# Deformable-convolution kernel: hats eight rows behind their offsets, the search for far pixels between the last hats, and another order at sampling's start

## The chip, the cores and the metric

The kernel runs on one core of one Trainium2 chip. The metric is the device time of one execution in microseconds (us), the median of several executions. The engines are TensorE (PE: matmuls and transposes; PEld is its weight load), VectorE (DVE), ScalarE (ACT), GpSimd (POOL) and SyncE (SP, which here only issues transfers, reads a register and branches). Each engine works through its own queue of instructions in order; an instruction that waits holds up everything behind it in the same queue. The kernel is written with a tile framework: a tile belongs to a tag with a number of buffers, and an instruction that writes a reused buffer waits until the last reader of the old contents is done. When a pool is closed and another takes its space, the first users of the new one wait for the last users of the old.

## The reference

`x` is `[2, 256, 128, 128]` in float32. Two residual blocks follow one another:

```
x = x + L0(gn(x))           # gn: GroupNorm with 32 groups
x = x + L1(gn(x))

L0(x):  for dil in (1, 9, 12):
            off = conv3x3(x, w_off, 18 channels, dilation dil)
            y   = sum over 9 taps k of w_def[c,k] *
                  bilinear(x, at pixel + tap k * dil + off[k])   # 0 outside
            branch = gelu(layernorm over channels(y) * bw + bb)
        out = ln(sum of branches + conv1x1(x) + b)
        out = ln(mlp(out) + out)                      # 256 -> 512 gelu -> 256
L1(x):  conv3x3(x, ternary weights) + bias
```

The offsets are small for the data at hand but may be anything: a sampled point further than two pixels from its tap's place is a far pixel and must still come out right.

## The kernel before

**Statistics and phase A** (0 to about 938 us). For each of the two images, its GroupNorm statistics are taken (L529), then `phase_a` (L321) goes over 32 groups of R = 4 rows. `columns(g)` loads the rows (`xa`, issued on ACT's queue, L340), normalises them on the DVE (L207), transposes them on PE (L350), copies them out of PSUM on ACT (L355), stores them as a zero-padded table in DRAM for sampling (SP, L356), multiplies them by all taps of the three offset convolutions (`pz`, PE, L364) and copies the product into a ring of 40 rows (`zr`, L371; the rows alternate between DVE and ACT). As soon as the ring holds the rows that eight rows of offsets need (twelve further down, the largest dilation), `offsets(G)` adds the taps up on the DVE (`zs`, L398 to L412), shifts and sums them on PE (`po`, L415), copies the offsets out (`offs`, L423), subtracts the usual position (`rest`, L425), keeps the largest distance per column and row (`reach`, L428), stores the offsets (SP, L432) and splits them into three bf16 parts (`parts`, L438 to L441; two buffers, by G's parity). Then `make_hats` runs twice, once for every four rows: eight PE transposes of `parts` (`pp`, L450 and L451), two DVE copies (`planes`, L453 and L454), and six times a pair of matmuls (`ph`, L463, two PSUM banks) followed by an absolute value on ACT (`hb`, L470); after every three of them a DVE operation makes hat functions of them (L474) and SP stores them to the DRAM tensor `hats` (L475, one store of 576 KB and one of 720 KB; `hb` has three buffers). At the bottom of an image the last step of the ring brings several `offsets` with two make_hats each behind the last columns.

**The search** (`missing`, L558 to L727; 938 to 965 us) has a pool of its own. It loads tables (`aux`, `misc`, `tapid`), marks the pixels whose `reach` is over two (`V`, L580), ranks them by matmuls (`pb`, L591; `pl`, L606), and gathers three things for up to 128 of them by indirect DMA on POOL: their offsets (`of`), the vertical base positions of their row (`ybase`) and the horizontal ones of their column (`xbase`), all at L628. A long chain of small DVE operations (L644 to L724) finds the taps that the hats don't cover. If there are more of them than a fixed number, a flag is raised: `worst` is reduced over the partitions on POOL (L792), compared (L794), read into a register (L795, `beyond`), and a branch chooses between `sample_near` and a slow general path.

**Sampling** (`sample_near`, L1224; 966 to 5762 us). Its order is written out by hand: `pin` keeps an instruction in its place in the program. 396 units (image, one of 66 pairs of rows, branch) are worked through. `load_tiles` loads eleven `xs` tiles from the table for a pair of rows (L1269, 18 buffers), `load_hats(u)` loads up to three pairs `hy`, `hx` of unit u (L1295, three buffers each), `build` multiplies a pair into the interpolation matrix `A` (DVE, L1315), `sample` multiplies `xs` by `A` on PE (`pm`, L1416), ACT copies the product out (`ev`, L1428) and the DVE adds it up in a ring (L1377). `prepare(u)` builds all of unit u and then asks for the hats of unit u + 1; `sample(u, 1)` calls `prepare(u + 2)`. Image rows at the top edge have fewer taps, so units 0 to 2 have one pair of hats each and matmuls of 72 columns, later ones up to three pairs and 216. `lacking` (L729) computes what far pixels need in addition: ten indirect gathers on POOL (`G` and `dws`, L628), and some thirty DVE operations that multiply them by weights and add them up into `extra` (L735 to L771). Its result is first used when the first group of finished rows goes into the tail of layer 0.

The second block's convolution (5762 to 6694 us) is not touched.

The order at sampling's start, which the change alters, is in the code:

```
load_tiles(*units[0][0:2])
load_hats(0)
prepare(0)
prepare(1)
tail.extra = lacking(pool, tail.tile, miss)
begun_groups = 0
spot(0)
for u, (b, Rt, br) in enumerate(units):
```

Of the kernel before, what the change touches and what calls it, by code (L numbers as in the profile page):

```python
# [71 lines left out]
def conv_preact_kernel(ctx: ExitStack, tc: tile.TileContext, t: dict, out: bass.AP):  # L72
# [248 lines left out]
    def phase_a(b, pool, psum, k, beside):  # L321
# [53 lines left out]
        def offsets(G):  # L375
# [60 lines left out]
            parts = k["parts"][G % 2]  # L436
# [47 lines left out]
        for g in range(NGRP):  # L484
            columns(g)
            next(beside, None)
            while G < H // ZG and min(H - 1, G * ZG + ZG - 1 + max(DILS)) < (g + 1) * R:
                parts = offsets(G)
                for j in range(ZG // R):
                    make_hats(G * (ZG // R) + j, parts, j * R)  # L490
                G += 1

    with ExitStack() as actx:
        psum = actx.enter_context(tc.tile_pool(name="ps_a", bufs=1, space=PSUM))

        def gps():
            return psum.tile([P, 512], F32, name="gnps", tag="tp", bufs=2)

        ap = actx.enter_context(tc.tile_pool(name="apool", bufs=1))
        dxs = sorted({d * s for d in DILS for s in (-1, 0, 1)})  # L500
        k = {
            "dxs": dxs,
            "zero": ap.tile([P, C], F32, name="zero"),
            "wz": ap.tile([P, KC, NZ], F32, name="wz"),
            "shift": ap.tile([P, len(dxs), P], F32, name="shift"),
            "mid": ap.tile([P, ZG, NOFF], F32, name="mid"),
            "hatw": ap.tile([P, 2, NTAP * NH], BF16, name="hatw"),
            "parts": [ap.tile([P, 2, ZG, P], BF16, name=f"parts{i}") for i in range(2)],
            "zr": ap.tile([P, ZRING, NZ], F32, name="zr"),
            "planes": [ap.tile([P, 2, NG], BF16, name=f"planes{i}") for i in range(2)],  # L510
        }
        nc.vector.memset(k["zero"], 0.0)
        for parts in k["parts"]:
            nc.vector.memset(parts, 0.0)
        XT = min(4, NGRP)
        beside = store_signs(ap)
        for b in range(NB):
            stats = ap.tile([P, KC, NGRP, 6], F32, name=f"stats1_{b}", tag=f"stats1_{b}")
            for c in range(KC):
                for g0 in range(0, NGRP, XT):  # L520
                    xt = ap.tile([P, XT * NG], F32, name="xt", tag="xt", bufs=3)
                    nc.sync.dma_start(
                        xt,
                        x[b, c * P : (c + 1) * P].rearrange("p h w -> p (h w)")[
                            :, g0 * NG : (g0 + XT) * NG
                        ],
                    )
                    for j in range(XT):
                        nc.vector.bn_stats(stats[:, c, g0 + j, :], xt[:, j * NG : (j + 1) * NG])  # L529
            if b == 0:  # L530
                load_now()
                nc.sync.dma_start(k["wz"], t["wz"].rearrange("(k p) n -> p k n", p=P))
                nc.sync.dma_start(k["shift"], t["shift"])
                nc.sync.dma_start(k["mid"], t["mid"])
                hatw = ap.tile([P, 2, NTAP * NH], F32, name="hatw32", tag="xt", bufs=3)
                nc.sync.dma_start(hatw, t["hatw"])
                nc.vector.tensor_copy(k["hatw"], hatw)
                split_rows(ap)
                pattern = ap.tile([P, NG], F32, name="pattern", tag="xt", bufs=3)
                nc.sync.dma_start(pattern[HALF : HALF + NPAT], t["pattern"])  # L540
                for pl in k["planes"]:
                    nc.vector.tensor_copy(
                        pl[HALF : HALF + NPAT, 1, :], pattern[HALF : HALF + NPAT]
                    )
            mean, rstd = group_norm(stats, f"gn1_{b}", gps)
            gn1.append((mean, rstd))

            nc.vector.tensor_scalar(negmean[b], mean, -1.0, None, ALU.mult)
            for c in range(KC):
                nc.vector.tensor_scalar(  # L550
                    convs[b][:, c, :], convs[b][:, c, :], rstd[:, c : c + 1], None, ALU.mult
                )
            phase_a(b, ap, psum, k, beside)
        for _ in beside:
            pass


    def missing(psum, pool):  # L558
# [4 lines left out]
        def bank(name):  # L563
            return psum.tile([P, 512], F32, name=name, tag="ms", bufs=2)

        aux = pool.tile([P, NB * H + ROWS + P], F32, name="aux", tag="aux", bufs=1)
        nc.sync.dma_start(aux, t["aux"])
# [3 lines left out]
        misc = const.tile([P, 16], F32, name="misc")  # L571
        nc.sync.dma_start(misc, t["misc"])
        thirds, own_w, seq = misc[:, 0:3], misc[:, 3:4], misc[:, 4:12]
        tapid = pool.tile([P, NTAP], F32, name="tapid", tag="tapid", bufs=1)
        nc.sync.dma_start(tapid, t["tapid"])

        V = tmp("V", P, NB * H)
# [21 lines left out]
        what = pool.tile([P, 8, 2], F32, name="what", tag="what", bufs=1)  # L599
        nc.vector.tensor_copy(what[:, :, 0], top)  # L600
        nc.vector.tensor_copy(what[:, :, 1], own_w.broadcast_to([P, 8]))
        pl = bank("pl")
        for j in range(8):
            one = pool.tile([P, ROWS], F32, name="one", tag="one", bufs=2)
            nc.vector.tensor_scalar(one, slot, rank[:, j : j + 1], None, ALU.is_equal)
            nc.tensor.matmul(  # L606
                pl[0:ROWS, 0:2], lhsT=one, rhs=what[:, j, :], start=j == 0, stop=j == 7
            )
# [27 lines left out]
        gather(base[:, 0], t["ybase"], 1)  # L636
        gather(base[:, 1], t["xbase"], 2)
# [91 lines left out]
    def lacking(pool, tile_v, m):  # L729

        def quarters(name):
            return tile_v(name).rearrange("p k n -> p (k n)").rearrange("p (j c) -> p j c", c=C)

        D = quarters("D")[:, 0:3]
        nc.vector.memset(D, 0.0)  # L735
        Gs = [quarters("G") for _ in range(EACH)]
        dws = quarters("dws")
        for j in range(EACH):
            for i in range(4):
                m["gather"](Gs[j][:, i], tables, i, m["idx"][:, j])  # L740
            m["gather"](dws[:, j], t["defwt"], 4, m["idx"][:, j])
        for j in range(EACH):
            s = dws[:, EACH + j]
            for i in range(4):
                w = m["got"][:, j, i : i + 1]
                if i == 0:
                    nc.vector.tensor_scalar(s, Gs[j][:, i], w, None, ALU.mult)
                else:
                    nc.vector.scalar_tensor_tensor(s, Gs[j][:, i], w, s, ALU.mult, ALU.add)
# [474 lines left out]
    def sample_near(pool, psum, k):  # L1224
# [235 lines left out]
        for u, (b, Rt, br) in enumerate(units):  # L1460
            if br == BRS[0] and u + len(BRS) < len(units):
                load_tiles(*units[u + len(BRS)][0:2])
            for c in range(KC):
                sample(u, c)
# [463 lines left out]
```

## Time and profile before

| | us |
|---|---|
| runs: median (lowest to highest of 3) | 6704.66 (6697.62 to 6708.94) |
| the profiled execution | 6696.33 |
| its span | 6694.5 |
| PE busy | 6292.8 (94%) |
| DVE busy | 5911.4 (88%) |
| ACT busy | 4194.8 (63%) |
| POOL busy | 686.2 (10%) |
| hats stores, 64 of each size | 576 and 720 KB each |
| granted clock, mean | 0.971 of full speed |

The durations quoted come from the one profiled execution, whose own time lies 8.3 us under the median of the three runs. The span is the time from its first to its last instruction. A busy share is a mean over stages that have different limits, so the stages are looked at one by one. Behind each group of instructions the profile gives the idle time of its engine just before them, and the instruction or the transfer that ended it. "SPq" is the queue of transfers that SP issues: a row there is the time of issuing, and the landing comes later.

### The profile page before, as it was taken

What the parts mean: (1) busy time and instruction counts of PE and PEld (TensorE: products, weight loads), DVE (VectorE), ACT (ScalarE), POOL (GpSimd) and SP (SyncE); (2) the same over time, 40 slices, a digit from 0 to 9 for tenths busy, and PEclk for the clock granted to TensorE, in tenths of its full rate; (3) what the DMA queues carried; (4) which work ended last, traced back from release to release, by engine and by line L of the source; (5) the groups of instructions that cost most, each with busy time, mean ns of one, the idle gap of its engine ahead of it and who ended that gap; (6) DMA issues with size and microseconds to landing.
All of it is one profiled execution on the core that took longest, in us unless ns stands there. A gap on an engine that the chain in (4) does not pass through costs nothing.

```text
span 6694.5 us, 100612 instructions
## 1 busy us (share of the span) xinstructions
PE 6292.8 (94%) x32242; PEld 4996.0 (75%) x32242; DVE 5911.4 (88%) x13758; ACT 4194.8 (63%) x8690; POOL 686.2 (10%) x667
## 2 busy tenths in 40 slices
PE   5889968899999999999999999999999999989999
PEld 3455548888888888888888888888888888744444
DVE  7766657999999999999878999999999999689996
ACT  2334427677777777777676777777777777545442
POOL 0000010011111111111110111111111111200000
PEclk9999978999999999999999999999999999889999
DMA  8866657887777877787667787778777777343332
GB/s 294 258 198 191 198 147 197 224 222 224 223 218 216 225 218 220 219 223 216 190 190 203 220 225 221 220 216 222 224 219 220 218 222 210 120 161 132 131 144 89
DMA packets 635571, 1360.47 MB, mean 203 GB/s; under 512 B 109336, under 2 KB 290120, under 8 KB 618512
## 3 DMA queue, kind: packets, MB, share of 16 engines
q1 hardware_dynamic: 617040, 1318.90, 68.6%
q10 hardware_dynamic: 17408, 33.56, 1.5%
q8 instruction: 261, 4.28, 0.3%
q14 instruction: 286, 2.34, 0.1%
q0 software_dynamic: 576, 1.39, 0.1%
HBM read 1087.09 MB, written 266.47 MB: 202 GB/s over the span
## 4 chain that ended last, share of the span: by engine, by line
PE 56%; DVE 26%; DMA 8%; ACT 6%; issue 3%; SPq 1%; POOL 0%; ACTq 0%; DVEq 0%; POOLq 0%
PE pm L1416 25%; DVE ring L1377 11%; PE hp L857 6%; PE pc L1755 6%; PE h L1100 5%; PE pz L364 4%; DVE A L1315 4%; DMA xa<-in_x 3%; PE pc L1100 3%; DMA hx<-hats 3%; ACT ev L1428 3%; ACT v L1078 2%; PE ph L463 2%; PE tp L872 2%; DMA xs<-tables 1%
## 5 line engine op out<-in xcount | busy, mean ns | idle before, releaser
L1416 PE MATMUL pm<-A,xs 96*128 96x216 f32 (+2 forms) x17424 | 3237.6, 342 | 196.3 <-DMA xs<-tables 47.0
L1416 PEld LDWEIGHTS pm<-A,xs 96*128 96x128 f32 x17424 | 3041.3, 194 | 392.1 <-ACT ev L1428 118.2
L1377 DVE SCALAR_TENSOR_TENSOR ring<-ev,defw,ring 128x256 f32<-128x256 f32 (+4 forms) x6372 | 2482.2, 451 | 101.4 <-ACT ev L1428 51.1
L1428 ACT COPY ev<-pm 128x432 f32<-128x432 f32 (+4 forms) x4488 | 1988.2, 483 | 903.5 <-PE pm L1416 672.4
L1315 DVE TENSOR_TENSOR A<-hy,hx 96x768 f32<-96x768 f32 (+1 forms) x1124 | 1008.8, 945 | 155.7 <-PE pm L1416 83.5
L1070 POOL TENSOR_TENSOR rs<-rs,mhalf 128x4 f32<-128x4 f32 x320 | 469.1, 1466 | 4214.6 <-DVE rs L1069 3667.6
L1755 PE MATMUL pc<-cring,signs 128*128 128x512 bf16 x3456 | 758.2, 382 | 17.1 <-DMA signs<-signd 7.7
L1078 ACT ACTIVATE v<-v,rs 128x256 f32<-128x256 f32 x1280 | 694.5, 594 | 16.9 <-POOL rs L1071 16.8
L1755 PEld LDWEIGHTS <-signs 128*128 128x128 bf16 x3456 | 339.7, 98 | 434.9 <-issue 28.2
L857 PE MATMUL hp<-S,w 128*128 128x512 f32 x1024 | 504.0, 618 | 0.6 <-ACT S L1180 0.6
L1064 DVE BATCH_NORM_STATS2 st<-v 128x6 f32<-128x256 f32 x1280 | 447.0, 411 | 38.0 <-ACT v L888 38.0
L1100 PE MATMUL h<-w,hT 128*128 128x256 f32 x2048 | 477.1, 379 | 0.0
L364 PE MATMUL pz<-wz,xa 128*128 128x486 f32 x1024 | 465.0, 583 | 8.5 <-DVE zr L371 8.5
L1359 ACT ACTIVATE ring<-ev,defw 128x256 f32<-128x256 f32 (+1 forms) x856 | 404.5, 485 | 24.2
L1100 PEld LDWEIGHTS h<-w,hT 128*128 128x128 f32 x2048 | 369.3, 190 | 65.5 <-issue 1.0
L470 ACT ACTIVATE hb<-ph 96x512 f32<-96x512 f32 (+1 forms) x384 | 214.0, 593 | 185.1 <-PE ph L463 170.0
L888 ACT COPY v<-tp 128x512 f32<-128x512 f32 x384 | 207.8, 598 | 184.7 <-PE tp L880 184.1
L1189 ACT ACTIVATE hT<-hp,b 128x512 f32<-128x512 f32 x256 | 176.0, 687 | 222.6 <-PE hp L857 219.8
L857 PEld LDWEIGHTS hp<-S,w 128*128 128x128 f32 x1024 | 200.4, 201 | 143.2 <-issue 127.3
L364 PEld LDWEIGHTS pz<-wz,xa 128*128 128x128 f32 x1024 | 187.8, 193 | 155.5 <-issue 129.7
L1100 PE MATMUL pc<-convw,xn 128*128 128x256 f32 x1024 | 271.4, 393 | 2.6 <-ACT xn L1161 2.6
L1100 PEld LDWEIGHTS pc<-convw,xn 128*128 128x128 f32 x1024 | 170.5, 191 | 73.1 <-ACT xn L1161 39.0
(242 smaller groups left out, 5058.6 us busy)
## 6 DMA issues: line engine op xcount, KB each, us to landing
hy<-hats SPq DMA_DIRECT2D x1112, 288.0 KB
hx<-hats SPq DMA_DIRECT2D x1112, 288.0 KB
xs<-tables SPq DMA_DIRECT2D x1452, 96.0 KB
g12d<-v SPq DMA_DIRECT2D x128, 512.0 KB
other<-g12d SPq DMA_DIRECT2D x128, 512.0 KB
hats<-hb SPq DMA_DIRECT2D x64, 720.0 KB
hats<-hb SPq DMA_DIRECT2D x64, 576.0 KB
xa<-in_x ACTq DMA_DIRECT2D x64, 512.0 KB
```

The costliest lines, as they stand in the source:

```text
L364: nc.tensor.matmul(pz[:, 0:NZ], lhsT=xt[:, c, r, :], rhs=k["wz"][:, c, :], start=c == 0, stop=c == KC - 1,)
L857: nc.tensor.matmul(out, lhsT=w, rhs=v, start=i == 0, stop=i == n - 1)
L1064: pin(nc.vector.bn_stats(st[:, j, :], rows[j]))
L1070: nc.gpsimd.tensor_tensor(rs[:, 0, :], rs[:, 0, :], mhalf[:, 0:n], ALU.pow)
L1078: nc.scalar.activation(row, row, func, scale=rs[:, 0, j : j + 1], bias=rs[:, 1, j : j + 1])
L1100: nc.tensor.matmul(bank[:, j, :], lhsT=v[:, px], rhs=w, start=False, stop=i == len(pairs) - 1,)
L1315: nc.vector.tensor_tensor(dst, hy[:, i0:i1].rearrange("p i t w -> p t i w"), hx[:, i0:i1].rearrange("p i t w -> p t i w"), ALU.mult,)
L1359: pin(nc.scalar.mul(dst, src, w))
L1377: pin(nc.vector.scalar_tensor_tensor(dst, src, w, dst, ALU.mult, ALU.add))
L1416: nc.tensor.matmul(pv[:, j, :, m0:m1, :], lhsT=xts[b, Rt][t][:, c * P : (c + 1) * P], rhs=A[:, y0:y1, m0:m1, AO + t * CI : AO + (t + 1) * CI],
L1428: nc.scalar.copy(dst.rearrange("p m (t j) -> p t m j", j=CI), pm[:, 0 : len(ts), 0:n].rearrange("p t (m j) -> p t m j", j=CI),)
L1755: nc.tensor.matmul(pc, lhsT=signs[:, k, (h * 3 + t) * 3 + kx, m * P : (m + 1) * P], rhs=xc[:, i, k, t * JC : (t + 1) * JC, kx : kx + W], s ...
```

## The change

It touches four things.

1. *Hats behind their offsets.* `offsets(G)` no longer runs its two `make_hats` at once: it puts them into a queue, `todo`, that is handed from one image to the next. After each `offsets` the queue is worked off down to four entries, and one more entry is run after each group of rows if over two are left. So hats are made one step of eight rows later. Behind the last `offsets` of the last image the rest of the queue is left standing. `parts` has three buffers in place of two.
2. *The search* moves into phase A's pools. It runs behind the last columns, with the remaining `make_hats` behind it in the program; the framework interleaves them. Its tables (`list_tables`) are loaded when the second image's statistics are done, into a buffer of the tag `xt`. Two of the three gathers are gone: `xbase` goes through the ranking matmul (`pl` has 56 columns in place of 2), and `ybase` is computed from a small table, the row and its parity. The reduction to the flag is a function, `reduce_worst`. `one` has three buffers in place of two.
3. *The flag's comparison and read* stand behind the remaining hats in the program.
4. *Sampling's start.* `load_hats(0)` comes before `load_tiles`, the table `count` is loaded behind `prepare(1)`, and `lacking` comes behind unit 1, its DVE operations pinned there.

```diff
@@ offsets
-            parts = k["parts"][G % 2]
+            parts = k["parts"][(b * (H // ZG) + G) % len(k["parts"])]
@@ phase_a
                 parts = offsets(G)
                 for j in range(ZG // R):
-                    make_hats(G * (ZG // R) + j, parts, j * R)
+                    todo.append((make_hats, (G * (ZG // R) + j, parts, j * R)))
                 G += 1
+                if G == H // ZG and b == NB - 1:
+                    return
+                while len(todo) > 2 * (ZG // R):
+                    run_first(todo)
+            if len(todo) > ZG // R:
+                run_first(todo)
+
+    def run_first(todo):
+        make, args = todo.popleft()
+        make(*args)
@@ missing
-        aux = pool.tile([P, NB * H + ROWS + P], F32, name="aux", tag="aux", bufs=1)
-        nc.sync.dma_start(aux, t["aux"])
+        aux, misc, tapid, what, ylist, V = tabs
...
-                pl[0:ROWS, 0:2], lhsT=one, rhs=what[:, j, :], start=j == 0, stop=j == 7
+                pl[0:ROWS, 0 : 2 + 2 * NTAP], lhsT=one, rhs=what[:, j, :], start=j == 0, stop=j == 7
...
         gather(of, offs_all, 0)
-        gather(base[:, 0], t["ybase"], 1)
-        gather(base[:, 1], t["xbase"], 2)
+        odd = pool.tile([R_, 1], U32, name="odd_row", tag="odd_row", bufs=1)
+        oddf = tmp("odd_rowf", R_, 1)
+        nc.vector.tensor_scalar(odd, ai[:, 1:2], 1, None, ALU.bitwise_and)
+        nc.vector.tensor_copy(oddf, odd)
+        nc.vector.tensor_scalar(base[:, 0, 0:NTAP], ylist[:, 0], at[:, 1:2], None, ALU.add)
+        nc.vector.scalar_tensor_tensor(
+            base[:, 0, NTAP:], ylist[:, 1], oddf, ylist[:, 2], ALU.mult, ALU.add
+        )
+        nc.vector.tensor_copy(base[:, 1], pl[0:R_, 2 : 2 + 2 * NTAP])
@@ new function
+    def list_tables(pool):
+        sizes = (NB * H + ROWS + P, NTAP, 3 * NTAP, 2 * NTAP, 8 * (2 + 2 * NTAP), NB * H)
+        all_ = pool.tile([P, sum(sizes)], F32, name="lists", tag="xt", bufs=3)
...
+        for dst, src in (
+            (aux, "aux"), (misc, "misc"), (tapid, "tapid"), (ylist, "ylist"), (xb, "xbase")
+        ):
+            nc.sync.dma_start(dst, t[src])
+        nc.vector.tensor_copy(what[:, :, 1], misc[:, 3:4].broadcast_to([P, 8]))
+        for j in range(8):
+            nc.vector.tensor_copy(what[:, j, 2:], xb)
@@ the stage around phase A
-            "parts": [ap.tile([P, 2, ZG, P], BF16, name=f"parts{i}") for i in range(2)],
+            "parts": [ap.tile([P, 2, ZG, P], BF16, name=f"parts{i}") for i in range(3)],
...
+            if b == NB - 1:
+                tables_m = list_tables(ap)
...
-            phase_a(b, ap, psum, k, beside)
+            phase_a(b, ap, psum, k, beside, todo)
         for _ in beside:
             pass
+        miss = missing(psum, ap, tables_m)
+        ids = miss["ids"]
+        farall = reduce_worst(miss["worst"])
+        while todo:
+            run_first(todo)
         flag = const.tile([P, 1], I32, name="flag")
         nc.vector.tensor_scalar(flag, farall, 0.0, None, ALU.is_gt)
         beyond = nc.values_load(flag[0:1, 0:1], min_val=0, max_val=1)
@@ sample_near
-        nc.sync.dma_start(count, t["count"].partition_broadcast(P))
...
+        load_hats(0)
         load_tiles(*units[0][0:2])
-        load_hats(0)
         prepare(0)
         prepare(1)
-        tail.extra = lacking(pool, tail.tile, miss)
+        nc.sync.dma_start(count, t["count"].partition_broadcast(P))
...
             for c in range(KC):
                 sample(u, c)
+            if u == 1:
+                tail.extra = lacking(pool, tail.tile, miss, pin)
```

The orders of PE, ACT and POOL in sampling and behind it are the same in both kernels. In the built order of the changed kernel SP reads the flag ahead of the last eight hats stores (the last four make_hats), and the DVE's `pos` (L644 of the kernel before), which waits for the gather, has one make_hats' operations (`planes` and two L474) behind it that stand ahead of the flag. In sampling the first four `xs` loads that wait for buffers stand behind the first of unit 3's three hats pairs; before, they stood behind all three.

## The prediction

> **What bounds the kernel now.** I read the page's busy shares first: TensorE (PE) 94% of 6694.5 us, the DVE 88%. The sampling and the second convolution, 5700 us of it, keep their instruction order but for sampling's first fifty or so, so only three places matter: the stage that makes tables and hats (phase A), the search for far pixels behind it, and sampling's start. The windows by stage come next. Columns: the stretch, its length, then busy time and count of PE, PE's weight loads, DVE, ACT and POOL, the granted clock, the DMA share and GB/s.
>
> ```profile
> 50.00:270.00 220.00, 186.24 (x735) 106.22 (x736) 169.97 (x362) 70.84 (x131) 1.34 (x2) 0.95 0.84 257
> 515.00:905.00 390.00, 370.23 (x1596) 211.82 (x1595) 240.48 (x459) 163.28 (x301) 0.00 (x0) 1.00 0.67 190
> 905.00:938.30 33.30, 20.02 (x98) 11.08 (x98) 17.01 (x32) 13.76 (x24) 0.00 (x0) 0.82 0.73 195
> 938.30:965.00 26.70, 4.47 (x18) 4.21 (x18) 14.78 (x103) 0.00 (x0) 3.59 (x4) 0.50 0.08 14
> 965.00:989.30 24.30, 0.00 (x0) 0.00 (x0) 6.98 (x25) 0.00 (x0) 14.51 (x12) 0.50 0.70 174
> ```
>
> Phase A is PE-bound in the second image (95% busy) and held by loads too in the first (85%). From 938.3 to 989.3 us every engine is nearly idle: that hole is what the change can win. Next, what PE waits for in phase A: the groups by form up to 968 us (count, then busy and mean; behind the second bar the idle time before them and what ended it).
>
> ```profile
> L415 PE MATMUL po<-zs,shift 128*128 128x144 f32 x576 | 84.1, 292 | 24.7 <-DVE zs L412 23.0 <-DVE offs L423 1.7
> L450 PE MATMUL pp<-ident_b,parts 128*128 128x128 bf16 x256 | 44.6, 226 | 30.1 <-DVE parts L440 30.1
> L451 PE MATMUL pp<-ident_b,parts 128*128 128x128 bf16 x256 | 41.4, 226 | 1.6 <-DVE parts L441 1.6
> ```
>
> Then the timeline of the hole (start, length, engine, line; in brackets the wait before it and what ended it).
>
> ```profile
> 914.45 18.59 SPq L475 DMA_DIRECT2D hats<-hb  x8
> ...
> 938.38 0.29 DVE L580 TENSOR_SCALAR V<-reach 128x256 f32<-128x256 f32 x1 [5.69 <-DMA hats<-hb]
> ...
> 949.77 1.29 POOL L628 DMA_INDIRECT of<-offs_all,ai  x1 [445.95 <-issue]
> 951.37 0.95 POOL L628 DMA_INDIRECT base<-in_ybase,ai  x1 [0.30 <-issue]
> 952.63 0.94 POOL L628 DMA_INDIRECT base<-in_xbase,ai  x1 [0.30 <-issue]
> 955.82 0.22 DVE L644 TENSOR_TENSOR pos<-of,base 128x54 f32<-128x54 f32 x1 [7.09 <-DMA base<-in_xbase,ai]
> ...
> 964.12 0.40 POOL L792 PARTITION_ALL_REDUCE farall<-worst  x1 [10.55 <-DVE worst L790]
> ...
> 968.76 7.88 SPq L1269 DMA_DIRECT2D xs<-tables  x11
> ...
> 976.69 0.59 SPq L1295 DMA_DIRECT2D hy<-hats  x1
> ...
> 988.36 0.43 DVE L750 TENSOR_TENSOR dws<-dws 128x256 f32<-128x256 f32 x1 [3.43 <-DMA dws<-in_defwt,idx]
> 988.71 0.55 DVE L1315 TENSOR_TENSOR A<-hy,hx 96x384 f32<-96x384 f32 x1
> ```
>
> It reads as one chain: the last hats land (938.2), the search runs (to the flag, 964.7), SP reads the flag and queues eleven `xs` and only then the first hats; the first build (L1315) stands on the DVE behind `lacking`'s wait for its gathered weights. The first sampling matmul is at 989.31.
>
> **Phase A.** Now the transposes of `parts` (L450, L451) start as soon as `offsets` has them, so PE stands for 30.1 + 1.6 = 31.7 us until the DVE has split them; eight rows later they are long done. By windows, 9.3 of the L450 waits lie in the second image and 19.7 in the first, 1.1 outside my windows. I take all of the second image's and half of the first's, where the DMA share is 0.84 and the DVE waits 93.2 us for `xa` (L207), so that time won may be lost to the next load: 9.3 + 9.9 = 19 us. Bounds: none to 31.7; a loss is possible only if the hats, now between a group's columns, make waits of their own (first rival). The `po` waits (24.7) stay. The third `parts` buffer costs nothing.
>
> **Work pushed back.** Before, the last `zr` copy ends at 900.2 and 28 `hb` activations (L470), that is 28/6 = 4.67 make_hats, follow; after, at most 7 do. The 2.33 more are not saved, only done later, so the columns end 2.33 × 3.3 us (12 `ph` matmuls at some 0.22 apart, 16 transposes at 0.055, in the quiet stretches of the timeline) = 7 us earlier. Last columns: 900.2 − 19 − 7 = 874, called T.
>
> **Tail.** The last offsets' `reach` is ready 9.7 us behind the last `zr` (909.9 − 900.2). From V (938.38) to the flag (964.70) is 26.3. Out of it go the wait for `aux` (1.2, L583; its loads now come at the second image's start, five issues and nine small copies under a DVE that is busy 240 of 390 us) and two gathers (2 × (0.95 + 0.30) = 2.5). The matmul that carries `xbase` is 56 columns wide in place of 2: nothing if narrow width is free, 3.2 at most (16 records at 0.36 us against 0.56, a 128-column f32 transpose at half clock); I take 1. The DVE copies for `ybase` lie under the gather's 3.4 us landing. Two make_hats interleaved on the DVE ahead of the flag cost 2 × (0.42 + 0.41 + 2 × 0.95) = 5.5. So the flag comes at T + 9.7 + 26.3 − 1.2 − 2.5 + 1 + 5.5 = T + 38.8. In SP's queue its read stands ahead of the last eight hats stores: all eight wait for the search. The read and its way take 2 us, the eight stores go 2.65 apart (18.59 for eight, with 932.72 the last), which is 18.6, and the last needs 5.5 to land (932.72 to 938.21). Hats landed: T + 38.8 + 26.1 = 939, where it was 938.2. So phase A's gain is spent on standing in SP's queue: what is late next is the store, not PE.
>
> The gather's landing is the unsure term: 3.4 us in the quiet search (DMA share 0.08), while sampling's first gathers, beside loads (0.70), needed 7.4: 4 us more at worst, and DVE's `pos` (L644) stands in front of hats' L474. The Trainium skill ("DMA: Bandwidth & Descriptors", section Queues, rings and completion order) says that each DMA engine takes turns between its queues packet by packet, which speaks against a gather hidden for nothing beside 576 and 720 KB stores, and the two landings agree with it; by that rule the flag would be up to those 4 us later, and the net 4 smaller.
>
> **From the last hats to the first matmul.** Search (26.3), the branch behind it (2.9), `count`, eleven `xs` ahead of hats (968.36 to 976.69) and `lacking`'s waits leave the path. What stays, since the pool is reused and so waits for the last store: issue of `hy` and `hx` 1.2, landing 4.3 (an `hx` issued at 1039.46 released the DVE at 1043.73), the build 0.55. The two memsets of `A` on POOL (4.81) run beside that landing, and would set the start if it were shorter. First matmul 939 + 6.1 = 945, against 989.3: −44.
>
> **Given back at sampling's start.** `lacking` issues some 16 us of DVE work (L749, six for 2.9; L758, six for 2.7; L769 to L771 for 3.9; the rest 6). Before, only its last half lay behind the first build; now all of it stands behind unit 1 in the queue that makes PE's next `A`. In 989.3 to 1021 the DVE is busy 20.2 of 31.7 us, so half is hidden there, and half, 8, delays PE. Second, before, all three hats pairs of unit 3 stood ahead of the four `xs` at 1013.47, which wait for PE to give buffers back; now two pairs stand behind such a wait. That is the pattern that already starves PE at unit 6:
>
> ```profile
> 1036.31 2.46 SPq L1269 DMA_DIRECT2D xs<-tables  x4
> ...
> 1043.73 0.96 DVE L1315 TENSOR_TENSOR A<-hy,hx 96x768 f32<-96x768 f32 x1 [7.70 <-DMA hx<-hats]
> ```
>
> I price it at 6, between nothing and this 7.7. Sum: −44 + 8 + 6 = −30. The profiled execution took 6696.33 (6694.5 span and 1.8 around it), so its like afterwards is 6666. It stands 8.3 under the median of the runs shown, 6704.66, which by the same sum becomes 6674.
>
> The clock: after the hole it stays at 0.50 from 938.3 to 1021, through 31.7 us in which PE is busy. The skill ("TensorE: Matmul & The Clock Gate", Part 1: The HAM clock gate) has full rate back after some 3.4 us of sustained work; by it, units 0 to 2 would be half as long, in both kernels. The row decides: I keep 0.50 for the narrow first units, and the same length for them in both.
>
> **Rivals.** (1) *Slower: hats starve PE between columns.* `ph` has two banks; an ACT `hb` copy takes 0.59 where two `ph` matmuls take some 0.43, and in the tail, where nothing lies between, they go 0.64 apart: 6 × 0.21 = 1.3 us per make_hats. It decides from (30 + 13)/1.3 = 33 of the 64 calls on; with all 64, 83 − 30 = +53, 6758. For it: L463 waits for L470 for 6.0 us already. Against: the order now puts `pz` and transposes between. (2) *Phase A gives little, or the flag comes late*, by 10 to 19 us, and hats land that much later, one for one: −11 to −20, some 6690. For it: all of the tail hangs on one queue. Against: phase A's `parts` waits are plain rows. (3) *Nothing is given back*: `lacking` finds idle DVE, and hats for unit 3 come in time, 6660. For it: PE at 0.50 leaves slack in units 0 to 2. Against: unit 6's row above. That the change does nothing is out: the first hats no longer stand behind the search.
>
> **How the numbers follow.** Forecast 0.58, rival 2 0.20, rival 3 0.15, rival 1 0.07. A measurement of this kernel tells 0.2% (13.4 us) from nothing. The forecast's own bounds: phase A 19 less or 12.7 more, give-back 6 to 14 less or 2 more; not all at once, so 6655 to 6692. With rival 3 below, rival 2 above and some 6 us of scatter between runs the range is 6648 to 6696. Faster: 0.58 + 0.15 + two thirds of rival 2 = 0.86; within: the rest of rival 2, 0.07; slower 0.07.
>
> **What would show it.** Right: no L450 wait of note; last `zr` near 874; SP waiting for the flag near 913, then eight stores end to end; last landing near 938; first matmul near 945 with `lacking` behind unit 1; PE idle some 6 to 10 us more between there and 1000. Wrong: `ph` waiting for `hb` in rows (rival 1), hats landed past 950 (rival 2), unit 6 as far ahead as unit 0 (rival 3).

## The result

The changed kernel takes 6654.54 us (median of five runs, 6642.81 to 6657.68), against 6708.94 (five runs, 6697.62 to 6712.47): ratio 0.9918, 95% interval 0.9904 to 0.9933, so 54 us less. The forecast was 6674 (30 us less than the 6704.66 shown), the range 6648 to 6696. The profiled execution took 6654.54, its span 6652.5; the one of before, 6696.33, lay some 12 us under the median of its kernel, so the two traces show only 42 of the 54 us.

PE's groups in the changed kernel up to 920 us, as columns before: count, busy, mean, then idle time before them and what ended it.

```profile
L364 PE MATMUL pz<-wz,xa 128*128 128x486 f32 x1024 | 463.5, 580 | 28.1 <-DVE zr L371 28.0
L415 PE MATMUL po<-zs,shift 128*128 128x144 f32 x576 | 81.2, 289 | 6.5 <-DVE zs L412 4.6 <-DVE offs L423 1.7
...
L450 PE MATMUL pp<-ident_b,parts 128*128 128x128 bf16 x256 | 37.9, 223 | 0.0
```

The wait for `parts` is gone to the last tenth, as forecast. The wait of `po` has shrunk too, from 24.7 us to 6.5, which was not; and `pz` now waits 28.1 us where it waited 8.5 in the kernel before:

```profile
L364 PE MATMUL pz<-wz,xa 128*128 128x486 f32 x1024 | 465.0, 583 | 8.5 <-DVE zr L371 8.5
```

The second image is now all PE:

```profile
50.00:270.00 220.00, 189.35 (x761) 107.80 (x762) 178.12 (x379) 70.13 (x130) 1.34 (x2) 0.98 0.86 262
...
484.00:851.00 367.00, 361.22 (x1577) 209.71 (x1576) 234.34 (x454) 160.73 (x301) 0.00 (x0) 1.00 0.69 201
851.00:889.00 38.00, 24.47 (x127) 16.50 (x126) 31.25 (x141) 11.15 (x20) 1.69 (x2) 0.81 0.42 116
889.00:920.00 31.00, 14.84 (x64) 7.37 (x62) 13.68 (x30) 12.59 (x22) 4.44 (x2) 0.72 0.71 208
```

These are its windows by stage: 361 of 367 us busy in the second image's columns (before 95%), then the search beside hats (to 889), then the last hats alone. Of the empty hole of 50 us, 12.5 are left: PE stands from 907.6 to 920.1, while the last hats are stored and the first loads land. Now the DVE's timeline of the tail and of sampling's start (the changed kernel's lines: `pos` L588, flag L780, hats L474, build L1347, `lacking` L790 to L826):

```profile
878.17 0.22 DVE L588 TENSOR_TENSOR pos<-of,base 128x54 f32<-128x54 f32 x1 [1.72 <-DMA of<-offs_all,ai]
...
888.88 0.15 DVE L780 TENSOR_SCALAR flag<-farall 128x1 int32<-128x1 f32 x1 [0.21 <-POOL farall L688]
...
908.24 0.96 DVE L474 TENSOR_SCALAR hb<-hb 120x1536 f32<-120x1536 f32 x1 [1.31 <-ACT hb L470]
...
919.31 0.56 DVE L1347 TENSOR_TENSOR A<-hy,hx 96x384 f32<-96x384 f32 x1 [1.60 <-DMA hx<-hats]
932.78 0.95 DVE L1347 TENSOR_TENSOR A<-hy,hx 96x768 f32<-96x768 f32 x1 [12.91 <-DMA hx<-hats]
...
959.01 1.66 DVE L1347 TENSOR_TENSOR A<-hy,hx 96x768 f32<-96x768 f32 x2 [12.61 <-DMA hx<-hats]
...
961.66 0.70 DVE L790 MEMSET D<- 128x768 f32 x1
...
976.54 1.02 DVE L824 SCALAR_TENSOR_TENSOR extra<-part,misc,extra 128x768 bf16<-128x768 bf16 x1
...
978.35 1.82 DVE L1347 TENSOR_TENSOR A<-hy,hx 96x768 f32<-96x768 f32 x2
```

The seventh build of the kernel before:

```profile
1020.01 0.95 DVE L1315 TENSOR_TENSOR A<-hy,hx 96x768 f32<-96x768 f32 x1 [5.14 <-PE pm L1416]
```

The first build comes 69.4 us earlier than before (988.71), the seventh (978.35, before 1020.01) only 41.7: two waits of 13 us for hats and then `lacking` stand between them. SP's queue shows why the hats are late:

```profile
885.33 24.22 SPq L475 DMA_DIRECT2D hats<-hb  x10
915.95 0.66 SPq L1327 DMA_DIRECT2D hy<-hats  x1
916.66 0.57 SPq L1327 DMA_DIRECT2D hx<-hats  x1
917.28 6.99 SPq L1301 DMA_DIRECT2D xs<-tables  x11
924.31 0.59 SPq L1327 DMA_DIRECT2D hy<-hats  x1
...
950.52 2.85 SPq L1301 DMA_DIRECT2D xs<-tables  x4
953.47 0.54 SPq L1327 DMA_DIRECT2D hy<-hats  x1
```

Unit 1's pair stands behind eleven tiles, and unit 3's second pair behind four tiles that wait for PE.

Step by step, where T is the end of the last `zr` copy:

| step | forecast | trace after |
|---|---|---|
| T (before 900.2) | 874 | 850.9 |
| flag (888.88) | T + 38.8 | T + 38.0 |
| last hats landed (pool free at 915.6) | T + 64.9 | T + 64.7 |
| first matmul behind that | 6.1 | 4.5 |
| first matmul, against 989.31 | -44 | -69.3 |
| given back by the 41st build | 14 | 18.8 |

A second profile of the changed kernel has the flag at T + 38.5, the last hats at T + 67.2, the first matmul 69.4 us earlier and 16.7 us given back.

### The profile page after: what moved, and what is told of

The parts are those of the page before. It is cut to its first block, busy times and chain, and to the rows that moved or that the text cites. A ratio compares the mean times of both kernels' runs of the same rounds, so it can differ in the third digit from the quotient of the medians.

```text
span 6652.5 us, 100588 instructions
## 1 busy us (share of the span) xinstructions
PE 6295.0 (95%) x32242; PEld 5006.0 (75%) x32242; DVE 5907.6 (89%) x13772; ACT 4194.8 (63%) x8690; POOL 687.1 (10%) x665
## 4 chain that ended last, share of the span: by engine, by line
PE 54%; DVE 28%; DMA 8%; ACT 6%; issue 3%; SPq 1%; POOL 0%; DVEq 0%; ACTq 0%; POOLq 0%
PE pm L1448 23%; DVE ring L1409 12%; PE hp L890 6%; PE pc L1789 6%; PE h L1133 5%; PE pz L364 4%; DVE A L1347 4%; DMA hx<-hats 3%; ACT ev L1460 3%; PE pc L1133 2%; DMA xa<-in_x 2%; ACT v L1111 2%; PE ph L463 2%; PE tp L905 1%; DVE st L1097 1%
## 5 line engine op out<-in xcount | busy, mean ns | idle before, releaser
L1409 DVE SCALAR_TENSOR_TENSOR ring<-ev,defw,ring 128x256 f32<-128x256 f32 (+4 forms) x6372 | 2481.2, 451 | 98.1 <-ACT ev L1460 52.1
L1347 DVE TENSOR_TENSOR A<-hy,hx 96x768 f32<-96x768 f32 (+1 forms) x1124 | 1010.3, 945 | 180.3 <-DMA hx<-hats 100.2
L364 PE MATMUL pz<-wz,xa 128*128 128x486 f32 x1024 | 463.5, 580 | 28.1 <-DVE zr L371 28.0
L371 ACT COPY zr<-pz 128x486 f32<-128x486 f32 x128 | 72.3, 565 | 260.0 <-PE pz L364 257.3
```

The source lines that it names most:

```text
L364: nc.tensor.matmul(pz[:, 0:NZ], lhsT=xt[:, c, r, :], rhs=k["wz"][:, c, :], start=c == 0, stop=c == KC - 1,)
L1347: nc.vector.tensor_tensor(dst, hy[:, i0:i1].rearrange("p i t w -> p t i w"), hx[:, i0:i1].rearrange("p i t w -> p t i w"), ALU.mult,)
L1409: pin(nc.vector.scalar_tensor_tensor(dst, src, w, dst, ALU.mult, ALU.add))
```

## The experiments

Gains below are ratios to runs of the kernel before on the same chip, with their 95% intervals. A time within sampling is compared from the first sampling matmul on, since T scatters by some 10 us between executions.

**The lag alone.** In the kernel before, the queue of make_hats, worked off before the search, and the third buffer:

```diff
-                    make_hats(G * (ZG // R) + j, parts, j * R)
+                    todo.append((make_hats, (G * (ZG // R) + j, parts, j * R)))
...
+        while todo:
+            run_first(todo)
```

> The kernel before with the queue of make_hats and the third parts buffer alone: hats eight rows behind their offsets, all of them done ahead of the search, which stays where it was, as does sampling's start. Theory A (a wait in phase A costs its own length and then a stretch at half clock): the last zr copy comes near 851 us, as in the changed kernel, against 900.2 before; 2.33 more make_hats stand behind it, at two stores 2.6 us apart each, so the last hats land near 938.2 - 49 + 12 = 901 and everything later keeps its distance: some 37 us faster than before, ratio 0.9945. Half-clock time of the first image near 10 us, against 31. Rival (the waits alone, as I forecast them): last zr near 874, hats near 924, 14 us faster, ratio 0.998. Rival B (the gain in phase A came from the search's move): last zr near 900, no change or 12 us slower.

Measured: 6665.09 us, ratio 0.9945 (0.9928 to 0.9963), as theory A's sum has it. From the first to the last `zr` copy it takes 783.3 us, the changed kernel 783.2, the kernel before 832.3: the whole 49 us of phase A are the lag's. Of the groups up to 912 us:

```profile
L364 PE MATMUL pz<-wz,xa 128*128 128x486 f32 x1024 | 465.8, 583 | 21.0 <-DVE zr L371 21.0
L415 PE MATMUL po<-zs,shift 128*128 128x144 f32 x576 | 81.5, 291 | 9.1 <-DVE zs L412 7.2 <-DVE offs L423 1.7
L450 PE MATMUL pp<-ident_b,parts 128*128 128x128 bf16 x256 | 38.0, 224 | 0.0
```

The same picture as in the changed kernel: `po` waits less here too. But theory A's reason falls. The granted clock stood at 0.50 for 27.3 us of the first image's columns, hardly under the 30.7 before, and in the changed kernel for 13.7, at the same length. The clock is not what made the wait dear.

**The rest without the lag.**

```diff
-                    todo.append((make_hats, (G * (ZG // R) + j, parts, j * R)))
+                    make_hats(G * (ZG // R) + j, parts, j * R)
```

> The changed kernel with make_hats run at once behind each offsets: the moved search, one gather and the new start without the lag. Theory A: the last zr near 900, L450 waits near 30 us and half-clock time in the first image near 30 us again; last hats land near 938; the search runs beside the last hats, so its flag comes at 945 to 950 and the first matmul near 950, 39 us ahead of before, of which 20 to 27 are given back in units 0 to 3: 12 to 20 us faster than before, ratio 0.997 to 0.998. Together with the lag alone this makes 37 + 12 to 20 = 49 to 57, against the change's measured 54: the parts add. Rival (the parts overlap: with hats late the search is hidden anyway, or nothing): no gain here, ratio 1.000, or the whole gain, 0.992.

Measured: 6686.81, ratio 0.9979 (0.9966 to 0.9991). T is 897.6, L450 waits 29.1 and `po` 25.1 us again, the first matmul comes at 949.9 (39 us earlier) and the 13th build is 23 earlier. By ratio the parts make 0.55% and 0.21%, together 0.76%, beside 0.82% to 0.86% for the change.

**Half the lag**: hats one group of four rows behind.

```diff
+            if todo and not (b == NB - 1 and g == NGRP - 1):
+                run_first(todo)
             while G < H // ZG and min(H - 1, G * ZG + ZG - 1 + max(DILS)) < (g + 1) * R:
...
-                while len(todo) > 2 * (ZG // R):
+                while len(todo) > ZG // R:
                     run_first(todo)
-            if len(todo) > ZG // R:
-                run_first(todo)
```

> The changed kernel with hats one group of four rows behind their offsets, not two. Theory (a wait vanishes once the split of parts is done ahead of PE's transposes, and four rows, some 12 us of PE work, are enough): the last zr within 5 us of the changed kernel's 851, no L450 waits of note; fewer make_hats stand behind the last columns, and all twelve last stores go ahead of the flag's read, so the hats land near 851 + 40 = 891 to 900, the search ends near 895 to 900 and the first matmul comes near 905, against 920: 10 to 18 us faster than the changed kernel. Rival (the DVE's row of work needs the whole eight rows): L450 and po waits of 10 us or more come back, last zr at 860 to 870, and the kernel is no faster.

Measured: 6664.38, ratio 0.9939 (0.9925 to 0.9953), 14 us slower than the changed kernel by medians. The rival holds in its result, but the wait came back somewhere else. Groups up to 930 us:

```profile
L364 PE MATMUL pz<-wz,xa 128*128 128x486 f32 x1024 | 459.5, 587 | 46.7 <-DVE zr L371 46.4
L415 PE MATMUL po<-zs,shift 128*128 128x144 f32 x576 | 97.5, 290 | 1.1 <-DVE offs L423 1.0
L450 PE MATMUL pp<-ident_b,parts 128*128 128x128 bf16 x256 | 37.1, 222 | 0.0
```

No wait for `parts`, none for `po`, and 46.7 us of `pz` for the DVE's `zr` copies, 42 of them in the first image, whose columns take 418.1 us (before 420.3, with the full lag 391.0); the second image's take 366.1 as with the full lag. Where they come from, the timeline shows:

```profile
271.38 1.00 DVE L207 TENSOR_SCALAR xa<-xa,gn_mean,gn_rstd 128x512 f32<-128x512 f32 x2 [7.54 <-DMA xa<-in_x]
...
273.16 0.66 DVE L371 COPY zr<-pz 128x486 f32<-128x486 f32 x1
...
273.87 2.80 PE L364 MATMUL pz<-wz,xa 128*128 128x486 f32 x3 [6.80 <-DVE zr L371]
```

The DVE waits 7.5 us for the rows of the next columns (`xa`, L207), and the `zr` copy that PE needs is behind that in its queue. So it is with all eight `pz` waits of 2.8 us and more in the first image, 36 of its 42 us: the DVE had stood 3.3 to 7.5 us for `xa` less than 6 us before. Both lags run one make_hats per group, the half lag ahead of `offsets` and the full one behind it. Why the half lag meets longer stops (the DVE waits 73 us for `xa` in the first image, with the full lag 50) is not shown. And the last hats landed at T + 56, but T was 877.8.

**The gathers.** The changed kernel with three gathers and a two-column ranking matmul:

```diff
-        nc.vector.tensor_scalar(odd, ai[:, 1:2], 1, None, ALU.bitwise_and)
...
+        gather(base[:, 0], t["ybase"], 1)
+        gather(base[:, 1], t["xbase"], 2)
```

> The changed kernel with the three gathers back (offsets, row bases, column bases) and the 2-column ranking matmul. Theory (two gathers cost 1.25 us each on POOL ahead of the DVE's pos, minus what hats fill in): pos starts 2 to 3 us later, the flag too, the hats land 1 to 3 us later; against the changed kernel 1 to 4 us slower, which runs can hardly tell. Rival (beside hats stores each gather lands later, 7 us in place of 3): pos 6 us or more later, and as much at the first matmul.

Measured: 6654.55, ratio 0.9924 (0.9905 to 0.9943); the changed kernel beside it 6650.23, 0.9914 (0.9899 to 0.9929). Runs can't tell them apart. The DVE's timeline of this kernel can (flag L773, build L1340):

```profile
894.10 0.15 DVE L773 TENSOR_SCALAR flag<-farall 128x1 int32<-128x1 f32 x1 [0.21 <-POOL farall L681]
...
908.16 0.96 DVE L474 TENSOR_SCALAR hb<-hb 120x1536 f32<-120x1536 f32 x1 [1.56 <-ACT hb L470]
...
919.27 0.55 DVE L1340 TENSOR_TENSOR A<-hy,hx 96x384 f32<-96x384 f32 x1 [1.58 <-DMA hx<-hats]
```

T is 847.7. `pos`, the first operation behind the gathers, starts at T + 34.0, in the changed kernel's two profiles at T + 27.2 and T + 27.8: the rival's 6 us and more, though the landings take 5.0, 3.8 and 5.7 us from issue and not its 7 (3.1 to 3.4 in the quiet search of before). The flag comes at T + 46.4, 8 us later than in the changed kernel (T + 38.0 and T + 38.5). Yet the last hats operation starts at T + 60.4, which is within what the changed kernel shows (T + 57.3 and T + 60.2), and the first matmul at T + 72.2 (T + 69.1 and T + 71.7). SP's queue holds all hats stores ahead of the flag's read here. So the flag does not set the end of the tail, and nor did the one gather move it: in this kernel as in the changed one each store is issued within 0.1 us of its DVE operation. What comes last is the making of the hats.

**lacking**: put back ahead of the loop, left out, and on POOL.

```diff
+        tail.extra = lacking(pool, tail.tile, miss, pin)
         begun_groups = 0
...
-            if u == 1:
-                tail.extra = lacking(pool, tail.tile, miss, pin)
```

> The changed kernel with lacking put back ahead of the loop over units (still with its operations pinned). Its first DVE operations then wait for gathers that land around 925 to 941 us, in front of unit 2's build and the first ring additions. Theory: if lacking's place behind unit 1 saves what stands in front of the DVE, this is 5 to 12 us slower than the changed kernel, build 2 at 948 or later in place of 940.4. Rival (the price of lacking is the same wherever it stands, since its 16 us of DVE delay a build either way, and behind unit 1 it also pushes unit 3's hats behind four tile loads): within 4 us of the changed kernel, or a few us faster.

Measured: 6637.34, ratio 0.9913 (0.9893 to 0.9934): the rival. Builds 2 and 6 come 31.0 and 45.2 us behind the first matmul; in the changed kernel 20.4 and 58.3. With `lacking` out of the way early, SP's queue again holds unit 3's hats ahead of the tiles that wait, and they are there when the DVE gets to them.

```diff
-                tail.extra = lacking(pool, tail.tile, miss, pin)
+                tail.extra = pool.tile([P, 3, C], BF16, name="extra")
+                nc.vector.memset(tail.extra, 0.0)
```

> The changed kernel without lacking: its ten gathers and its 16 us of DVE work are left out, and zero is added for far pixels in its place. It prices the work that now stands behind unit 1. Theory (half of the 16 us is hidden, as I forecast): builds 6 on come 8 us earlier against builds 0 to 5, and the kernel is 6 to 10 us faster than the changed one beside it. Rival (nothing of it is hidden): 16 us faster. Rival B (all of it is hidden under PE's half clock): within 2 us.

Measured: 6630.06, ratio 0.9895 (0.9877 to 0.9913): 20 us under the changed kernel by medians, though the intervals overlap. The trace is plainer: build 6 comes 37.2 us behind the first matmul in place of 56.5 (the changed kernel's second profile). Some 3 of these 19 us are there already at builds 4 and 5 (34.3 and 35.5, against 37.2 and 38.3), ahead of `lacking`'s DVE work; the ten gathers are the only other thing left out. The other 16 are the DVE's. My half was wrong: all 16 us stand in PE's way at that place.

```diff
-                    pin(nc.vector.scalar_tensor_tensor(s, Gs[j][:, i], w, s, ALU.mult, ALU.add))
+                    ve.tensor_scalar(g, g, w, None, ALU.mult)
+                    ve.tensor_tensor(s, g, s, ALU.add)
...
```

(`ve` is POOL, `nc.gpsimd`; the other operations of `lacking` go there in the same way.)

> The changed kernel with lacking's arithmetic on POOL in place of the DVE, at the same place in the program. Theory (all 16 us stand on the DVE's path at the start, as leaving it out showed, and POOL is idle from 933 us until the first tail near 1040): the DVE's row is that of the kernel without lacking, build 6 comes 16 to 20 us earlier, and the kernel is some 16 us faster than the changed one, ratio 0.989 to 0.990. Rival (POOL's forty-odd operations take longer than until extra is first read near 1040, or slow the DVE down beside them): no gain, or PE waits for extra.

Measured: 6644.93, ratio 0.9906 (0.9889 to 0.9922), not told apart from the changed kernel. Build 6 does come 15 us earlier (41.0), but by build 20 only 6 are left (98.1 against 103.8).

**Tiles behind the samples.**

```diff
-            if br == BRS[0] and u + len(BRS) < len(units):
-                load_tiles(*units[u + len(BRS)][0:2])
             for c in range(KC):
                 sample(u, c)
+            if br == BRS[0] and u + len(BRS) < len(units):
+                load_tiles(*units[u + len(BRS)][0:2])
```

> The changed kernel with the tiles of the next pair of rows asked for behind the samples of unit u, not ahead, so that unit 3's three pairs of hats are issued ahead of the tile loads that wait for PE. Theory (the hats standing behind those loads cost some 10 us at the start: builds 4 and 5 at 959 and 960 behind a wait of 12.6 us): builds 4 and 5 come near 946, and the kernel is 5 to 12 us faster than the changed one, ratio to before 0.990 to 0.991. Rival (lacking's 16 us on the DVE stand there anyway, or the later tiles make PE wait in every third unit): no faster than the changed kernel, or slower by 10 us and more.

Measured: 6618.32 (6616.72 to 6621.78), ratio 0.9878 (0.9859 to 0.9896): some 25 us under the changed kernel by ratio, twice the most that I expected, and clearly faster than both kernels. Timeline of its start (a merged row shows the shape of its first instruction; the first 216-column matmul is at 955.8):

```profile
931.79 33.15 PE L1448 MATMUL pm<-A,xs 96*128 96x72 f32 x148 [1.13 <-issue]
...
946.68 2.29 DVE L1347 TENSOR_TENSOR A<-hy,hx 96x768 f32<-96x768 f32 x3 [2.32 <-PE pm L1448]
949.97 0.70 DVE L790 MEMSET D<- 128x768 f32 x1
...
964.85 1.02 DVE L824 SCALAR_TENSOR_TENSOR extra<-part,misc,extra 128x768 bf16<-128x768 bf16 x1
966.67 1.81 DVE L1347 TENSOR_TENSOR A<-hy,hx 96x768 f32<-96x768 f32 x2
967.23 23.08 PE L1448 MATMUL pm<-A,xs 96*128 96x216 f32 x134 [2.29 <-ACT ev L1460]
```

Unit 3's three builds are ready as expected; `lacking` starts 12 us earlier and ends at 965.9; PE has units 1 and 2 and the start of unit 3 to do meanwhile and stands for 2.3 us only, at its end. So the late hats and `lacking` are one price, not two: with the hats late, the DVE idles first and works at `lacking` when PE has nothing left.

**Unit 1's hats ahead of the first tiles too, all mends together, and PE kept busy.** The first of these, against the kernel with later tiles:

```diff
         load_hats(0)
-        load_tiles(*units[0][0:2])
         prepare(0)
+        load_tiles(*units[0][0:2])
         prepare(1)
```

> The kernel with later tile loads (unit 3's hats ahead of the tiles that wait for PE), and unit 1's pair of hats asked for ahead of the first eleven tiles as well. It prices the 12.9 us that build 1 waits for its hx in the changed kernel. Theory (that wait is on the path, for PE runs dry behind unit 0): build 1 comes 5 to 9 us earlier, at 926 to 929 counted from a last zr at 851, and the kernel is 3 to 8 us faster than with later tiles alone, ratio 0.987. Rival (unit 0 is held by its own eleven tiles, which now come 1.3 us later): within 2 us of it.

Measured: 6623.37, ratio 0.9874 (0.9858 to 0.9891), not told apart from later tiles alone (0.9878), so that the 3 to 8 us of the theory are neither shown nor excluded. Build 1 now stands 0.5 us ahead of the first matmul, where it stood 12.2 behind, but build 2 at 13.5 has gained 6.5, and build 6 at 42.1 only 2.7. PE's pauses in unit 0 end with `xs` tiles: unit 0 is held by its tiles, as the rival has it. By the 41st build, however, this execution is 7.3 us ahead of the one with later tiles, counted from the first matmul (153.8 against 161.1).

All mends together:

> All three mends of sampling's start together: unit 1's hats ahead of the first tiles, unit 3's ahead of the tiles that wait, lacking on POOL. Theory (the prices add: 10 us and more for the tiles, 3 to 8 for unit 1's hats, 16 for lacking): 30 to 40 us faster than the changed kernel, some 90 us faster than before, ratio 0.985 to 0.987. Rival (they overlap: PE at half clock is the next limit of units 0 to 2): no faster than with later tiles alone, 0.988.

Measured: 6623.83, ratio 0.9883 (0.9866 to 0.9899): the rival, nothing beyond later tiles. POOL's row costs the DVE much of what it takes off. Ring additions of the DVE from 942 to 1000 us, first with `lacking` on the DVE (unit 1's hats ahead), then with it on POOL:

```profile
L1409 DVE SCALAR_TENSOR_TENSOR ring<-ev,defw,ring 128x256 f32<-128x256 f32 x26 | 11.8, 480 | 0.4
```

```profile
L1412 DVE SCALAR_TENSOR_TENSOR ring<-ev,defw,ring 128x256 f32<-128x256 f32 x23 | 14.5, 656 | 0.3
```

With the other widths of this addition and the builds in the same 58 us, the DVE's own operations take some 10 us more, of the 16 us of `lacking` that it is spared.

And ten matmuls ahead of unit 0:

```diff
+            for _ in range(10):
+                nc.tensor.matmul(
+                    k["pm"][3].rearrange("p j n -> p (j n)"), lhsT=ones3,
+                    rhs=row3.rearrange("p j c -> p (j c)"), start=True, stop=True,
+                )
```

> The same, and ten matmuls of 512 columns of constants, whose result is thrown away, keep PE busy while the first hats are on their way. The traces so far show units 0 to 2 at half clock through some 32 us in which PE hardly stops. Theory A (the clock is low because PE stood still for 12 us ahead of unit 0): with these matmuls the clock is at 1.00 when unit 0 begins and stays there; units 0 to 2 take 16 us less and the kernel is 10 to 16 us faster than without them. Theory B (matmuls of 72 columns, each behind a weight load of 128, leave PE's array idle so much that the clock falls again): it is back at 0.50 within some 10 us of the first unit, and the kernel is within 3 us of the one without them.

Measured: 6628.32, ratio 0.9890 (0.9874 to 0.9907), within 5 us of the one without. It does not decide, for PE was not kept busy:

```profile
922.22 4.45 PE L1624 MATMUL pm<-row,ones 128*128 128x512 bf16 x10 [4.41 <-issue]
933.04 1.95 PE L1451 MATMUL pm<-A,xs 96*128 96x72 f32 x8 [6.37 <-DMA hx<-hats]
...
941.61 42.75 PE L1451 MATMUL pm<-A,xs 96*128 96x72 f32 x214 [1.28 <-DMA xs<-tables]
```

The ten matmuls ran at half clock (0.43 us from start to start) and PE stood idle for 6.4 us behind them. The clock stayed at 0.50 until 972.3. Here too the rows are merged: from 941.6 to 965.5 PE is busy without a pause with matmuls of 72 columns (a few of 48), from 965.5 on with 216. What this says of theory B stands in the last section.

**The changed kernel again.**

> The changed kernel once more, on the chip of the runs beside it: ratio to before 0.990 to 0.993. It is the yardstick for the three others, and a second profile of it tells which differences within sampling belong to one execution (its profile lost 10 us between 1100 and 1400 us, at 37 us of half clock against 24 before).

Measured: 6650.23, ratio 0.9914 (0.9899 to 0.9929), with a first matmul at 919.9, 69.4 us ahead of before, and 52.7 of them left at the 41st build. This execution did not lose 10 us from there to the 161st (52.1), as the first one did (50.5 to 40.9), but had 46.0 left at the end, where the first one had 42.0. I put these losses down to neither kernel.

## Why the prediction came out as it did

*Phase A: right in kind, too small by half.* The step that failed is "The `po` waits (24.7) stay": they fell by 18, in the lag alone by 16 as well. `zs`, which `po` waits for, is DVE work queued behind hats (in the kernel before, a hats operation L474 ran in the 6 us ahead of every such wait); making hats later frees it too. "I take ... half of the first's" failed as well: with the full lag the first image gave back the whole `parts` wait. Against these stand 20 us of new `pz` waits, most of them in the first image; there each one of 1.6 us and more follows a stop of the DVE of 2.6 to 5.4 us for `xa`, which is the loss to the next load that the prediction allowed for. So idle time of PE up to T fell by 25; 9 us more are hats pushed back (716 recorded `ph` matmuls up to T, then 684, which is 2.67 make_hats at 3.3; the prediction's own parts, 12 × 0.22 and 16 × 0.055, make 3.5 each). The other 15 of the 49 us are shorter busy time that I can't break down: half clock fell by 17 us in the changed kernel, 8 us of work at most, but in the lag alone it hardly fell, and the stretch from the first to the last `zr` was as long: PE was busy 6.5 us longer there and idle 6.3 us less, so the half clock was made up for by shorter waits. The 49 us lie 10 beyond the most that the prediction had (26 and 12.7 more).

*Tail: the right sum for a wrong reason.* T + 64.9 met T + 64.7 (T + 67.2 in the second profile). But "In SP's queue its read stands ahead of the last eight hats stores: all eight wait for the search" did not happen: the read stood there, but it was over (890.4) 1 us before the DVE had finished the first of the eight (891.4). The stores went out as the DVE finished them, and with the flag 8 us later and behind all stores they ended at T + 67.7, within 3 us of both. What stood behind the search were the hats' own operations, in the DVE's order; the last eight went 2.5 us apart, close to the 2.65 of the row I had taken, and that is why the sum came out. The Trainium skill's rule on queues that take turns ("DMA: Bandwidth & Descriptors", section Queues, rings and completion order) fits the gather's landing of 4.5 and 5.1 us beside the stores against 3.4 before, but neither that nor the two gathers less reached the end.

*Given back: 18.8 (in the second profile 16.7) in place of 14 by the 41st build, and two terms that were one.* The forecast added 8 for `lacking`, half hidden, and 6 for unit 3's hats. Leaving `lacking` out, or asking for the hats ahead of the tiles, each took away most of the sum alone (1.3 and 5.8 us given back by the 41st build); `lacking` ahead of the loop did not by then (14.9). Not seen at all was unit 1's wait of 12.9 us behind eleven tiles; taking it away brought little.

*Rivals.* The slower one, `ph` waiting for ACT in every make_hats, did not come: PE waited 3 us for `hb` in all (before 6.0). The late flag came in two kernels made for other questions (T + 46.4 and, at half the lag, T + 46.8), but in both its read stands behind all stores; a late flag ahead of them, which is what this rival feared, was not tried, and the changed kernel has only that 1 us to spare. "Nothing is given back" is wrong, though the total came near it, since phase A's surplus paid for it: of the 54 us, some 37 are the lag's (0.9945) and 14 the rest's (0.9979). That the time still lies in the range is in part luck: phase A gave 23 us more than forecast, and the lower end had been set for this rival.

The version with later tile loads, 6618.32 us, beats both kernels.

## What to carry to other kernels

When an engine waits for a product of the same step, running one step behind also frees what was queued behind that product on the other engine: count the waits of the whole queue, not of the one tile. How long the lag must be has to be tried: at half the lag the wait had only moved to the next consumer, behind an engine that itself stood for a load. When a start is pulled forward, look at the order in which its loads are issued: tile loads that wait for buffers in front of the next unit's data cost some 25 us here, when leaving out the work that had been moved behind unit 1 gained 20.

## What the hardware showed beyond that

POOL's elementwise work slows the DVE beside it: a 128x256 ring addition took 656 ns with `lacking` on POOL and 480 without, so moving 16 us of work from one to the other gained nothing that lasted.

The granted clock followed the shape of the matmuls and not the pauses. At sampling's start it stayed at 0.50 while PE worked without a pause on matmuls of 72 columns (a few of 48): 28.2 us in the kernel before (989.3 to 1017.5) and 23.9 us in the last experiment (941.6 to 965.5). In all fourteen traces it rose to 1.00 only 3.7 to 6.8 us after the first matmul of 216 columns, whether PE had stood for 6 us just ahead of that one, as in the changed kernel (954.8 to 960.8), or not at all. Twice later, at the images' other edges, the columns go over to 72 again while the clock is at 1.00; in 26 of these 28 places it fell to 0.50 within 3.6 to 6.8 us. The first of them in the kernel before, with no pause of PE (columns as in the windows by stage; matmuls of 144 columns and others to 3310.9, then of 72):

```profile
3304.50:3310.90 6.40, 6.40 (x42) 5.39 (x40) 4.65 (x11) 3.82 (x10) 4.71 (x1) 1.00 0.44 124
3310.90:3315.30 4.40, 4.36 (x39) 4.18 (x37) 4.22 (x9) 3.98 (x15) 0.00 (x0) 1.00 0.50 140
3315.30:3319.00 3.70, 3.70 (x19) 3.70 (x19) 3.52 (x15) 2.31 (x9) 0.42 (x1) 0.50 0.52 156
```

So the half clock of units 0 to 2 comes with the narrow matmuls (theory B), and the 0.50 that the prediction kept for them held in every trace. By the falls from 1.00, keeping PE busy ahead of them could win no more than their first few us. The Trainium skill ("TensorE: Matmul & The Clock Gate", Part 1: The HAM clock gate) gives 3.4 us of sustained work for the full clock; the rise behind the wide matmuls fits that, the 24 and 28 us of narrow ones at 0.50 do not. What it is about a 72-column matmul that does not count is open.
